# Attention, feed-forward and state-space block: weights in quarters, pinned statistics, an earlier decay rate, feed-forward tiles dealt out anew

## The chip, the cores and the metric

The kernel runs on one core of a Trainium2 chip. The metric is the device time of one execution in microseconds. The engines are TensorE (PE in the profile; PEld is its weight load), VectorE (DVE), ScalarE (ACT), GpSimd (POOL) and SyncE (SP), which issues every load and store of this kernel.

## The reference

Three residual branches are chained on x (4 x 256 x 512, so 1024 rows or eight tiles of 128), each behind a layer norm, and the feed-forward is used twice with the same weights:

```python
x = x + attention(_layernorm(x), w_attn, w_proj, adapter_wte, gating)
x = x + ffn(_layernorm(x), weight, bias, centroids, assignments)
x = x + mixer(_layernorm(x), in_proj_w, conv_w, conv_b, dt_bias, A_log, D, norm_w, out_w)
x = x + ffn(_layernorm(x), weight, bias, centroids, assignments)
```

The attention has 32 heads of 16 channels, rotary queries and keys, a causal softmax, and ten adapter keys with a softmax of their own, scaled by a gate. The feed-forward selects rows and columns by clusters:

```python
dots = softmax(x @ centroids.T / 0.1, axis=-1)      # 64 clusters
hits = dots > 0.01
query_sel = any(hits, axis=1)                       # rows
row_sel = any(hits, axis=0)[assignments]            # columns, over all 1024 rows
out = where(query_sel[:, None] & row_sel[None, :], x @ weight.T + bias, 0)
```

The mixer projects to a gate and to x (8192 channels each), to B and C (8 groups of 128) and to dt (128 heads), applies a causal convolution of four taps and silu, runs a state-space recurrence with the decay rates `A = -exp(A_log)`, gates, normalises in eight groups and projects back.

## The kernel before

Every large float32 product is made as three products of a high and a low part. `split` makes the parts: an ACT copy (line 104, "CAST" in the profile) gives the high part, and a subtraction (line 105) on DVE or POOL the low part. `mm3` issues the three matmuls (lines 112, 113 and 114) for each 128-row slice of the contraction. A normalised tile is made in three steps: `stats` (BN statistics and their aggregate on DVE), `root` (a square root on ACT, a reciprocal on DVE), then `scale` and `turn` (four transposes on PE, whose result is split into `axs`). ACT loads a function table whenever it passes from Sqrt to Exp or back; such loads are instructions of their own.

**Start.** SP loads x's tiles 0 and 1, the constants and the weights of q, k and v, each in two loads of 512 KB, then the rest of x, the gate, the adapter's rows `wte` and wproj. `weights` loads and splits one matrix, q and k with DVE's low parts, v with POOL's. Ten matmuls on a tile of ones run meanwhile (`warmed`). `rotated` makes the rotary embedding: three DVE products (lines 281, 284 and 285) and a POOL sum (line 287), then POOL stacks high and low parts (lines 305 and 306) and PE transposes them (trp). The statistics of tiles 2 to 7 and their common root stand next in the program.

**Attention's blocks.** A loop runs over i = 0 to 31, four batches of eight blocks of four heads. PE's order is written by hand (`tc.manual_schedule`), one block being: scores sc of block i, steps of the coroutines that are due, the weighted values py of block i-2, the transposes ptr of block i-1, the gathering of block i-3. Coroutines yield a kind ("long", "turn" or "values") and a due block, and `step(kind, i)` moves those that are due. The other engines' orders come from a list scheduler; `keep_in_program_order` holds an instruction behind the one before it in the program on its engine, `issue_after` holds what follows behind a given instruction of the same engine, and `high_priority` pulls an instruction forward. The exponentials of a block (line 461) are 16 ACT instructions.

**The first feed-forward** starts inside the loop. `Feed.tile` makes a tile's two halves pd (288 columns each; the first has the 64 cluster logits), takes the maximum (lines 206 and 207), the exponentials fe (209), the hit (212), the row's choice (213), the maximum into `hits` (214) and the new row (217 to 219). The dictionary `FEEDS` deals the tiles out: tiles 0 to 2 enter at blocks 28, 29 and 31. Tiles 3 to 5 follow the loop, and tiles 6 and 7, the `late` ones, the last output projections po. Then `select` counts the hits over the rows with a matmul (cnt), makes the mask (msk), and eight `take` copies (line 230) put the new rows into x.

**The mixer's start.** Weight blocks `win` are fetched ahead and split (w). The decay rates `a_s` are loaded, and ACT and DVE make -exp of them (lines 807 and 808). Takes, statistics and roots (mrs, line 140) alternate; ACT normalises (mxn, line 150) and PE transposes. Then come dt, its cumulative sums, and 64 blocks of projections pp, convolutions, state-space products and, group by group, output projections pog.

**The end.** The same `Feed` class, named g, runs on the tiles as their last pog products come in, then select, the takes and the stores of the output.

Of the kernel before, what the change touches and what calls it, by code (L numbers as in the profile page):

```python
# [9 lines left out]
F32 = mybir.dt.float32  # L10
F32R = mybir.dt.float32r
# [9 lines left out]
P = 128  # L21
# [56 lines left out]
def hybrid_kernel(  # L78
# [17 lines left out]
    nc.vector.memset(eps, EPS)  # L96
    ones = keep.tile([P, P], F32, name="ones")
# [74 lines left out]
    class Feed:  # L172
# [24 lines left out]
        def tile(self, t, xs, halves):  # L197

            p2 = self.p2
            pa, pb = halves  # L200
            for j, o in enumerate(halves):
                mm3(o, [[v[:, k, :] for v in xs] for k in range(KC)],
                    [[v[:, k, j, :] for v in self.w] for k in range(KC)])
            small = lambda n, w: p2.tile([P, w], F32, name=f"{self.name}{n}", tag=f"f{n}")
            nm = small("nm", 1)
            nc.vector.tensor_reduce(nm, pa[:, :NCL], AX.X, ALU.max, negate=True)
            nc.vector.tensor_scalar(nm, nm, 10.0, None, ALU.mult)
            e, se = small("e", NCL), small("se", 1)
            nc.scalar.activation(e, pa[:, :NCL], AF.Exp, bias=nm, scale=10.0, accum_out=se)
            nc.vector.reciprocal(se, se)  # L210
            hit, sel = small("hit", NCL), small("sel", 1)
            nc.vector.tensor_scalar(hit, e, se, 0.01, ALU.mult, ALU.is_gt)
            nc.vector.tensor_reduce(sel, hit, AX.X, ALU.max)
            nc.vector.tensor_tensor(self.hits, self.hits, hit, ALU.max)
            new = self.new[:, t, :]
            m = FH - NCL
            nc.vector.tensor_tensor(new[:, :m], pa[:, NCL:], self.bias[:, :m], ALU.add)
            nc.vector.tensor_tensor(new[:, m:], pb, self.bias[:, m:], ALU.add)
            nc.vector.scalar_tensor_tensor(new, new, sel, x[:, t, :], ALU.mult, ALU.add)

        def select(self, cnt, rows):

            nc.tensor.matmul(cnt, self.hits, ones, start=True, stop=True)
            csel = self.p2.tile([NCL, P], BF16, name=f"{self.name}c", tag="fc")
            nc.vector.tensor_scalar(csel, cnt, 0.5, None, ALU.is_gt)
            nc.tensor.matmul(rows, csel, self.onehot, start=True, stop=True)
            self.mask = rows.bitcast(U32)
# [5 lines left out]
    def attention(later):  # L233
        with ExitStack() as es:
# [19 lines left out]
            def weights(w, src, tag, engine, pool=p2):  # L254
                for k in range(0, KC, 2):
                    r = pool.tile([P, 2, C], F32, name="ar", tag=tag)
                    load(r, src[:, k : k + 2, :])
                    for j in range(2):
                        split([v[:, k + j, :] for v in w], r[:, j, :], engine)
# [316 lines left out]
            def finished(b, c, po):  # L576
# [7 lines left out]
                if b == B - 1 or c == 1:  # L584
                    feed.norm.root(t if b == B - 1 else t - 1, t + 1)

            def fed(f, t):
                yield "turn", None
                with tc.high_priority(offset=60):
                    xs = normed(f.norm, t)  # L590
                yield "long", None
                f.tile(t, xs, [ps.tile([P, FH], F32, name="pd", tag="m") for _ in range(2)])
# [3 lines left out]
            load(x[:, 1, :], xv[:, 1, :])  # L596
# [3 lines left out]
            warmed(ps.tile([P, C], F32, name="warm", tag="m"), [ones] * 10)  # L600
# [3 lines left out]
            )  # L604
            for t in range(2):
                norm.stats(t)
            norm.root(0, 2)
            weights(wq_s, wq, "pc0", nc.vector)
# [5 lines left out]
            load(wte_s, wte)  # L614
            nc.gpsimd.tensor_copy(identb, ident)
# [17 lines left out]
            FEEDS = {28: 0, 29: 1, 31: 2}  # L633
# [18 lines left out]
            for t in range(2, TT):  # L652
                norm.stats(t)
# [8 lines left out]
            with tc.manual_schedule(engines={nc.tensor.engine}):  # L662
                for i in range(n):
# [8 lines left out]
                    if i in FEEDS:  # L672
                        moved(fed(feed, FEEDS[i]), i - 1)
                    if i == 3:
# [66 lines left out]
                late = {}  # L741
                for c, po in enumerate(pos):
                    t = 2 * b + c
                    finished(b, c, po)
                    late[t] = p2.tile([P, C], F32, name="axn", tag="t1")
                    feed.norm.scale(t, late[t])
                step("long", n + 3)
                for t, xn in late.items():
                    tr = ps.tile([P, KC, P], F32, name="tr", tag="m")
                    xs = [p2.tile([P, KC, P], F32R, name=f"axs{j}", tag=f"axs{j}") for j in range(2)]  # L750
                    feed.norm.turn(xn, tr, xs)
                    feed.tile(t, xs, [ps_s.tile([P, FH], F32, name="pd", tag="sc") for _ in range(2)])
# [4 lines left out]
    def mixer(feed, later):  # L757
        with ExitStack() as es, ExitStack() as inner:
# [8 lines left out]
            nc.gpsimd.memset(w0.tile([P, 8], F32, name="fill0"), 0.0)  # L767
# [37 lines left out]
            a_s = w1.tile([P, 1], F32, name="a_s")  # L805
            load(a_s, alog)
            nc.scalar.activation(a_s, a_s, AF.Exp)
            nc.vector.tensor_scalar(a_s, a_s, -1.0, None, ALU.mult)
# [7 lines left out]
            nc.gpsimd.memset(w1.tile([P, 32], F32, name="fill1"), 0.0)  # L816
# [488 lines left out]
```

## Time and profile before

| | us |
|---|---|
| median of 3 runs | 1895.22 |
| lowest and highest | 1891.03, 1895.73 |
| the profiled execution | 1896.1 |
| its span, first to last instruction | 1894.3 |
| PE busy | 1816.5 (96%) |
| DVE busy | 1465.8 (77%) |
| ACT busy | 1367.5 (72%) |
| POOL busy | 389.9 (21%) |

The times are device times of whole executions. The profile shows one of them, which took 1896.1; its span is 1.8 us shorter than its time. The page has the busy time of each engine, the span in forty slices with the clock that TensorE was granted, the chain of work that ended last, and groups of instructions. In the timeline, a row is start, length, engine, line, operation, output<-inputs, shapes and count; the bracket is the engine's idle time before it and what ended it. A window's row gives the busy time of every engine in a stretch and its granted clock, 1.00 being full speed.

### The profile page before, as it was taken

The page shows a single profiled execution, that of the slowest core. Times are in us where ns is not written, and L with a number is a line of the kernel's source. Part 1 is how long each engine was busy: PE and PEld are TensorE (multiplying, and loading weights), DVE is VectorE, ACT ScalarE, POOL GpSimd, SP SyncE. Part 2 cuts the span into 40 slices and gives each one's busy share as a digit, 9 for nine tenths or more (in the row PEclk, how much of TensorE's full clock was granted, in tenths as well). Part 3 has the DMA queues.
Part 4 walks back from the last instruction along what each step waited for, and adds up shares of the span by engine and source line. Part 5 has one row for each costly group of instructions (what it writes and reads, how often), then busy time and mean ns, then how long its engine had stood idle before and what let it go on. Part 6 is the DMA issues. An engine that isn't in the chain of part 4 may idle for free.

```text
span 1894.3 us, 29853 instructions
## 1 busy us (share of the span) xinstructions
PE 1816.5 (96%) x10690; PEld 1453.2 (77%) x10690; DVE 1465.8 (77%) x2319; ACT 1367.5 (72%) x2808; POOL 389.9 (21%) x380
## 2 busy tenths in 40 slices
PE   7999988799999999999999999999999999999997
PEld 6777767676777877877788778777787888787786
DVE  5566666688998778777877787778878877877777
ACT  4666675468998768777877787778777876786753
POOL 5432230011311212211112111211221221122100
PEclk8999999999999999999999999999999999999999
DMA  4000000125555454544544454545454545455341
GB/s 135 8 1 1 22 15 1 32 70 180 168 183 189 148 160 148 171 152 156 174 150 147 144 187 146 172 145 167 151 167 145 160 152 168 146 162 164 112 124 49
DMA packets 151908, 240.34 MB, mean 127 GB/s; under 512 B 12368, under 2 KB 77520, under 8 KB 151760
## 3 DMA queue, kind: packets, MB, share of 16 engines
q1 hardware_dynamic: 151760, 238.44, 39.4%
q8 instruction: 84, 1.38, 0.3%
q14 instruction: 64, 0.52, 0.1%
HBM read 202.75 MB, written 35.65 MB: 126 GB/s over the span
## 4 chain that ended last, share of the span: by engine, by line
PE 76%; ACT 8%; DVE 8%; DMA 3%; issue 3%; POOL 1%; SPq 0%; DVEq 0%; ACTq 0%; POOLq 0%
PE pp L112 12%; PE pp L113 11%; PE pp L114 11%; PE pyy L1021 8%; PE pog L112 6%; PE pog L114 6%; PE pog L113 6%; PE trx L1006 3%; ACT e L461 2%; DMA wor<-in_wout_dram 2%; DVE acc L947 1%; PE ptr L477 1%; PE pq L112 1%; PE pq L113 1%; PE pq L114 1%
## 5 line engine op out<-in xcount | busy, mean ns | idle before, releaser
L112 PE MATMUL pp<-mx,w 128*128 128x512 f32 (+1 forms) x1160 | 465.2, 401 | 8.1 <-DVE acc L947 7.6
L114 PE MATMUL pp<-mx,w 128*128 128x512 f32 (+1 forms) x1160 | 453.8, 391 | 0.0
L113 PE MATMUL pp<-mx,w 128*128 128x512 f32 (+1 forms) x1160 | 453.6, 391 | 0.0
L947 DVE SCALAR_TENSOR_TENSOR acc<-pp,cw_s,acc 128x1012 f32<-128x1012 f32 (+2 forms) x240 | 304.9, 1270 | 22.8 <-ACT acc L940 22.2
L995 DVE TENSOR_TENSOR em<-em,gm 128x1536 f32<-128x1536 f32 x128 | 227.9, 1780 | 94.4 <-ACT em L989 86.0
L112 PEld LDWEIGHTS pp<-mx,w 128*128 128x128 f32 x1160 | 218.3, 188 | 65.6 <-issue 10.4
L114 PEld LDWEIGHTS pp<-mx,w 128*128 128x128 f32 x1160 | 218.3, 188 | 45.4 <-issue 0.4
L1044 POOL TENSOR_TENSOR sq<-sq,acc 128x1024 f32<-128x1024 f32 x55 | 132.7, 2412 | 581.0 <-ACT acc L1043 581.0
L983 POOL TENSOR_SCALAR_AFFINE_SELECT r<-r 128x512 f32<-128x512 f32 x128 | 141.5, 1106 | 532.1 <-DMA r<-cumd 452.2
L113 PEld LDWEIGHTS pp<-mx,w 128*128 128x128 f32 x1160 | 218.5, 188 | 40.8 <-issue 0.7
L104 ACT CAST w<-wr 128x512 fp32r<-128x512 f32 x144 | 88.4, 615 | 186.9 <-PE pp L113 148.1
L112 PE MATMUL pog<-wo,gh 128*128 128x512 f32 x512 | 204.5, 399 | 0.0
L988 ACT ACTIVATE em<-r,col_t 128x128 f32<-128x128 f32 x512 | 165.0, 391 | 48.9 <-PE pyy L1021 46.8
L114 PE MATMUL pog<-wo,gh 128*128 128x512 f32 x512 | 200.2, 391 | 0.0
L113 PE MATMUL pog<-wo,gh 128*128 128x512 f32 x512 | 199.9, 390 | 0.0
L1021 PE MATMUL pyy<-em,xd 128*64 128x256 f32 (+1 forms) x2048 | 189.1, 329 | 3.2 <-DVE em L995 3.2
L1021 PEld LDWEIGHTS pyy<-em,xd 128*64 128x64 f32 x2048 | 134.0, 137 | 64.6 <-issue 21.4
L991 ACT ACTIVATE em<-r,col_t 128x128 f32<-128x128 f32 x512 | 166.5, 388 | 0.0
L979 DVE TENSOR_SCALAR em<-r,col_t 128x128 f32<-128x128 f32 x512 | 137.1, 327 | 12.6 <-PE pyy L1021 10.1
L1007 DVE TENSOR_TENSOR xd<-trx,dt_t 128x512 f32<-128x512 f32 x128 | 86.2, 682 | 54.4 <-PE trx L1006 54.2
L105 DVE TENSOR_TENSOR w<-wr,w 128x512 fp32r<-128x512 f32 x139 | 99.0, 713 | 34.3 <-ACT w L104 34.3
L461 ACT ACTIVATE e<-sc,nmx 128x256 f32<-128x256 f32 (+1 forms) x256 | 104.2, 442 | 20.8 <-DVE nmx L455 20.7
(287 smaller groups left out, 3193.0 us busy)
## 6 DMA issues: line engine op xcount, KB each, us to landing
wr<-in_win_dram SPq DMA_DIRECT2D x287, 256.0 KB, 2.8
r<-cumd SPq DMA_DIRECT2D x128, 512.0 KB, 4.1
spill<-gb SPq DMA_DIRECT2D x63, 512.0 KB, 2.8
gr<-spill SPq DMA_DIRECT2D x120, 256.0 KB, 3.5
wor<-in_wout_dram SPq DMA_DIRECT2D x64, 256.0 KB, 3.3
out_dram<-x SPq DMA_DIRECT2D x8, 256.0 KB, 2.3
x<-in_x_dram SPq DMA_DIRECT2D x1, 1536.0 KB, 10.9
gr<-spill SPq DMA_DIRECT2D x8, 192.0 KB, 2.8
```

The lines of the kernel that those rows point to most:

```text
L112: nc.tensor.matmul(o, lh, rh, start=(first and k == 0), stop=False)
L113: nc.tensor.matmul(o, lh, rl, start=False, stop=False)
L114: nc.tensor.matmul(o, ll, rh, start=False, stop=(last and k == n - 1))
L461: nc.scalar.activation(es_[c][:, 2 * j + pr, :], sc[:, j, :], AF.Exp, bias=nm[:, j : j + 1], accum_out=rs[:, c, h : h + 1],)
L947: nc.vector.scalar_tensor_tensor(av[:, :, d:], pv[:, :, : L - d], cw_s[:, ch, tap : tap + 1], av[:, :, d:], ALU.mult, ALU.add,)
L979: nc.vector.tensor_scalar(e[:, b, 2, :], rv[:, b, 1, :], col_t[:, h, b, 1:2], 0.0, ALU.subtract, ALU.min,)
L983: nc.gpsimd.affine_select(rv[:, :, 0, :], rv[:, :, 0, :], pattern=[[0, B], [1, P]], compare_op=ALU.is_ge, fill=-1e30, base=0, channel_mult ...
L988: nc.scalar.activation(e[:, b, 1, :], rv[:, b, 1, :], AF.Exp, bias=col_t[:, h, b, 2:3])
L991: nc.scalar.activation(e[:, b, 0, :], rv[:, b, 0, :], AF.Exp, bias=col_t[:, h, b, 0:1])
L995: nc.vector.tensor_tensor(e, e, gm, ALU.mult)
L1021: nc.tensor.matmul(py[d, b, k * P :], xd[:, 2 * b + k, d], es2[hh][:, b, 2 * k : 2 if k == 0 else 3, :].rearrange("p s i -> p (s i)"), sta ...
L1044: (nc.gpsimd if n < NB - 1 else nc.vector).tensor_tensor(sq, sq, x2, ALU.add)
```

## The change

The weights of q, k and v are loaded in quarters of 256 KB, q's ahead of x's tile 1. Sixteen warming matmuls stand for ten. Tiles 0 and 1 have a root each. The statistics of tiles 2 to 7 are held behind what precedes them on DVE, the rotary products. The decay rates are loaded with the first weights and made in block 2 (the negation on POOL). Feed tiles 0 to 2 enter with their products at blocks 30, 31 and 32, without priority. `Feed.tile` is cut in two, `products` and `chosen`. Of tiles 6 and 7 both roots come ahead of tile 5's exponentials, and tile 7's transposes lie between the halves of tile 6. The last tile's hit is no longer merged into `hits`; a second matmul adds it to the count. The small fillers keep their sum of 40 columns.

```diff
@@ class Feed
         def tile(self, t, xs, halves):
+            for j in range(2):
+                self.products(xs, j, halves[j])
+            self.chosen(t, halves)
+
+        def products(self, xs, j, o):
+            mm3(o, [[v[:, k, :] for v in xs] for k in range(KC)],
+                [[v[:, k, j, :] for v in self.w] for k in range(KC)])
+
+        def chosen(self, t, halves):
             p2 = self.p2
             pa, pb = halves
-            for j, o in enumerate(halves):
-                mm3(o, [[v[:, k, :] for v in xs] for k in range(KC)],
-                    [[v[:, k, j, :] for v in self.w] for k in range(KC)])
...
             nc.vector.tensor_scalar(hit, e, se, 0.01, ALU.mult, ALU.is_gt)
+            if t < TT - 1:
+                nc.vector.tensor_tensor(self.hits, self.hits, hit, ALU.max)
+            else:
+                self.last = hit
             nc.vector.tensor_reduce(sel, hit, AX.X, ALU.max)
-            nc.vector.tensor_tensor(self.hits, self.hits, hit, ALU.max)
...
-            nc.tensor.matmul(cnt, self.hits, ones, start=True, stop=True)
+            nc.tensor.matmul(cnt, self.hits, ones, start=True, stop=False)
+            nc.tensor.matmul(cnt, self.last, ones, start=False, stop=True)
@@ attention: weights
                     r = pool.tile([P, 2, C], F32, name="ar", tag=tag)
-                    load(r, src[:, k : k + 2, :])
+                    if pool is p1:
+                        load(r, src[:, k : k + 2, :])
                     for j in range(2):
+                        if pool is not p1:
+                            load(r[:, j, :], src[:, k + j, :])
                         split([v[:, k + j, :] for v in w], r[:, j, :], engine)
@@ attention: finished, fed
                 if b == B - 1 or c == 1:
-                    feed.norm.root(t if b == B - 1 else t - 1, t + 1)
+                    return feed.norm.root(t if b == B - 1 else t - 1, t + 1)
...
                 yield "turn", None
-                with tc.high_priority(offset=60):
-                    xs = normed(f.norm, t)
-                yield "long", None
+                xs = normed(f.norm, t)
+                yield "long", max(0, B * 8 + t - 2)
@@ attention: the start
             load(x[:, 0, :], xv[:, 0, :])
-            load(x[:, 1, :], xv[:, 1, :])
...
-            warmed(ps.tile([P, C], F32, name="warm", tag="m"), [ones] * 10)
+            warmed(ps.tile([P, C], F32, name="warm", tag="m"), [ones] * 16)
...
+            weights(wq_s, wq, "pc0", nc.vector)
+            load(x[:, 1, :], xv[:, 1, :])
             for t in range(2):
                 norm.stats(t)
-            norm.root(0, 2)
-            weights(wq_s, wq, "pc0", nc.vector)
+                norm.root(t, t + 1)
...
             load(wte_s, wte)
+            load(a_s, alog)
...
-            FEEDS = {28: 0, 29: 1, 31: 2}
+            FEEDS = {28: 0, 29: 1, 30: 2}
...
             for t in range(2, TT):
-                norm.stats(t)
+                norm.stats(t, tc.keep_in_program_order)
...
+                    if i == 2:
+                        nc.scalar.activation(a_s, a_s, AF.Exp)
+                        nc.gpsimd.tensor_scalar(a_s, a_s, -1.0, None, ALU.mult)
@@ attention: after the loop
-                late = {}
+                xns, xss = {}, {}
                 for c, po in enumerate(pos):
                     t = 2 * b + c
-                    finished(b, c, po)
-                    late[t] = p2.tile([P, C], F32, name="axn", tag="t1")
-                    feed.norm.scale(t, late[t])
-                step("long", n + 3)
-                for t, xn in late.items():
+                    rooted = finished(b, c, po)
+                    xns[t] = p2.tile([P, C], F32, name="axn", tag="t1")
+                    feed.norm.scale(t, xns[t])
+
+                def turned_late(t):
                     tr = ps.tile([P, KC, P], F32, name="tr", tag="m")
-                    xs = [p2.tile([P, KC, P], F32R, name=f"axs{j}", tag=f"axs{j}") for j in range(2)]
-                    feed.norm.turn(xn, tr, xs)
-                    feed.tile(t, xs, [ps_s.tile([P, FH], F32, name="pd", tag="sc") for _ in range(2)])
+                    xss[t] = [p2.tile([P, KC, P], F32R, name=f"axs{j}", tag=f"axs{j}") for j in range(2)]
+                    feed.norm.turn(xns[t], tr, xss[t])
+
+                with tc.issue_after(rooted):
+                    step("long", n + 3)
+                turned_late(TT - 2)
+                halves = {t: [ps_s.tile([P, FH], F32, name="pd", tag="sc") for _ in range(2)] for t in xns}
+                feed.products(xss[TT - 2], 0, halves[TT - 2][0])
+                turned_late(TT - 1)
+                feed.products(xss[TT - 2], 1, halves[TT - 2][1])
+                feed.chosen(TT - 2, halves[TT - 2])
+                feed.tile(TT - 1, xss[TT - 1], halves[TT - 1])
@@ mixer
-            a_s = w1.tile([P, 1], F32, name="a_s")
-            load(a_s, alog)
-            nc.scalar.activation(a_s, a_s, AF.Exp)
-            nc.vector.tensor_scalar(a_s, a_s, -1.0, None, ALU.mult)
```

More of the change, by code (lines that the diff above doesn't have):

```diff
@@ L96, in hybrid_kernel @@
     nc.vector.memset(eps, EPS)
+    a_s = keep.tile([P, 1], F32, name="a_s")
     ones = keep.tile([P, P], F32, name="ones")
@@ L766, in mixer @@
             rg_s = [w0.tile([P, TT], F32, name=f"rg{i}") for i in range(2)]
-            nc.gpsimd.memset(w0.tile([P, 8], F32, name="fill0"), 0.0)
             po_ = pool("mo", 2, **freed)
@@ L815, in mixer @@
             load(nw_s, nw)
-            nc.gpsimd.memset(w1.tile([P, 32], F32, name="fill1"), 0.0)
+            nc.gpsimd.memset(w1.tile([P, 40], F32, name="fill1"), 0.0)
             dh = w1.tile([P, NB], F32, name="dh")
```

## The prediction

> **What bounds the kernel now.** I read the summary first, then the forty slices with the granted TensorE clock, then the chain that ended last, and then, stage by stage, the windows table and the timeline of the few microseconds around each moved instruction.
>
> ```profile
> span 1894.3 us, 29853 instructions
> ...
> PE   7999988799999999999999999999999999999997
> ...
> PEclk8999999999999999999999999999999999999999
> ...
> PE 76%; ACT 8%; DVE 8%; DMA 3%; issue 3%; POOL 1%; SPq 0%; DVEq 0%; ACTq 0%; POOLq 0%
> ```
>
> TensorE (PE) is the bound. It is below 90% in the first slice, in slices 6 to 8 (about 237 to 379 us: attention's last blocks, the feed-forward, the mixer's start) and in the last. Over three quarters of the chain is PE, and from 400 to 1800 us it never starves (last row below). The change leaves the mixer's 64 blocks nearly alone: three neighbouring pairs swap order there. So it can win only in five places: start, blocks 28 to 32, end of attention, start of the mixer, last feed-forward. In four of them PE idles now and then runs on a halved clock (columns: window, length, busy time of PE, PEld, DVE, ACT, POOL with counts, granted clock, DMA share, GB/s):
>
> ```profile
> 316.60:320.00 3.40, 1.33 (x9) 0.62 (x6) 3.40 (x8) 3.40 (x18) 0.00 (x0) 1.00 0.00 0
> 320.10:326.80 6.70, 5.73 (x23) 5.51 (x24) 2.30 (x10) 1.32 (x4) 1.40 (x3) 0.50 0.00 0
> 358.00:364.60 6.60, 5.17 (x25) 4.94 (x26) 2.25 (x6) 2.68 (x6) 0.00 (x0) 0.74 0.01 2
> 374.70:388.30 13.60, 10.09 (x37) 7.83 (x37) 8.76 (x25) 8.83 (x14) 3.05 (x4) 0.50 0.21 58
> 400.00:1000.00 600.00, 589.41 (x3225) 469.32 (x3224) 506.20 (x686) 480.82 (x864) 126.74 (x84) 1.00 0.50 161
> ```
>
> PE was busy for 1.33 of 3.40 us, and the clock was 0.50 in the next two windows, where a 128x288 product takes 0.24 us a step instead of 0.13.
>
> **Part by part.**
>
> *Start (quarters, pinned statistics, decay rates): -2 us, between -3.5 and +1.* Now q's four ACT casts (615 ns each) follow two 512 KB loads, and the first q product starts at 11.43 behind ACT's axs. With quarters only one cast follows the last landing: axs comes near 10.2. The third wk product now stands early in PE's order, so about 0.5 to 1 us of this is kept. The wv loads go out at about 10.7 instead of 11.81, and POOL's wv halves end near 20.8 instead of 22.43. From there POOL's rotary sums are the chain:
>
> ```profile
> 29.93 1.27 POOL L287 TENSOR_TENSOR r<-t,t 128x512 f32<-128x512 f32 x1 [0.72 <-DVE t L285]
> ```
>
> The fourth sum waited 0.72 us for DVE, where three BN statistics (0.66 us each) had slipped in ahead of it; pinned, all six come behind it. The sum should start near 27.5. What is added in front of ACT's first exponentials (38.49 now): an Exp table load plus a_s, then two wp casts (1.2 us), then a Sqrt table load (1.28). ACT idled 2.50 us in that place, waiting for a transpose, and the root cannot run before the sixth statistic (near 32) anyway, so I cost them at nothing; without that cover they cost 1.2 + 1.28 = 2.5. One added wait deserves a name: those two casts wait for the load of wproj, which SP issues once DVE has made wt's low half (31.84 to 32.55 now, issue at 32.57, 3.6 us to landing). Behind them on ACT stand the root, the last key casts and all exponentials. In the new order wt's low half runs ahead of the fourth rotary product, near 25, so wproj lands near 29.5, before the casts' turn. Six more issues on SP cost 0.43 us each, beside transfers in flight; a_log's issue goes ahead of wproj's, beside that wait. POOL's negation of a_s (128x1) is put at 0.2 us ahead of the fourth sum, by DVE's 0.15 for the same operation now.
>
> A rule speaks against the quarters: the Trainium skill (DMA: Bandwidth & Descriptors, Bandwidth) says to batch transfers to 1 MiB or more, giving 32% efficiency at 64 KB and 78% at 1 MB. Put 256 KB midway at 55% of its 425 GB/s and 512 KB at 66% (my estimates from that page): 3 MiB then take 13.5 instead of 11.2 us, 2.3 lost, and the start is worth nothing. In the trace, queued transfers overlap: a 2 KB packet takes 84 ns, a 4 KB one 159, so two halves cost 5.7% more, about 0.4 us over 3 MB. I go by the packets; the rule sets the upper end.
>
> *Blocks 29 to 32 (feed tiles 0 to 2 at blocks 30, 31, 32): -3.5, between -6 and +1.*
>
> ```profile
> 321.07 0.61 PE L112 MATMUL pd<-fw,axs 128*128 128x288 f32 x1 [2.21 <-ACT axs L104]
> ...
> 355.22 1.28 ACT L209 ACT_TABLE_LOAD   x1 [3.41 <-DVE fnm L207]
> ...
> 359.05 0.40 PE L112 MATMUL pd<-fw,axs 128*128 128x288 f32 x1 [2.83 <-ACT axs L104]
> ...
> 371.21 0.40 PE L223 MATMUL cnt<-ones,fh 128*64 128x128 f32 x2 [1.47 <-DVE fh L214]
> ```
>
> Tile 0's 24 products (297.5 to 300.7) leave block 29, and block 30's exponentials come about 2.3 us earlier (306.90 to 304.6); block 31's come 3.0 earlier (316.74 to 313.8). Tile 1's 3.2 us of products now lie in block 31, where PE is busy 1.33 of 3.40. Tile 2's products then start near 319: with a full clock they end 4.8 us earlier than today's 327.2, on a cold one 2. Between them I take 3.5. The other table loads stay under DVE's maxima. Beyond that, pd holds two of the three "m" buffers until DVE reads them; ptr and try stand behind it, hence the bad end.
>
> *End of attention (roots of tiles 6 and 7 together, tile 7's transposes inside tile 6's products, last hit apart): -4.2, between -5.5 and -1.5.* On ACT now: Exp table, fe of tile 5 (356.52), Sqrt table (356.94 to 358.22), root 7, then axs of tile 6 at 358.43, for which PE waited 2.83 us since the transposes at 355.62. With both roots first, axs of tile 6 comes one table load earlier, 357.4 (-1.0). Later the Exp table load (362.43) and fe 6 stood before tile 7's axs (365.20), which now follows its transposes, put between the halves of tile 6; that and a PE gap short enough to keep the clock (1.5 us were lost at 0.24 a step) make pd7 end at 365.6 instead of 369.7. The maximum into hits (1.11 us, in line ahead of cnt) leaves the chain, for one extra accumulating matmul (0.2 us): about -0.5 more, less if the clock stays halved. Take of tile 0: 372.5 to about 368.
>
> *Start of the mixer (decay rates gone): -2.5, between -3.5 and -1.*
>
> ```profile
> 374.52 1.28 ACT L807 ACT_TABLE_LOAD   x1
> ...
> 377.06 1.28 ACT L140 ACT_TABLE_LOAD   x1
> ...
> 379.41 1.97 PE L163 MATMUL tr<-con,mxn 128*128 128x128 f32 x8 [2.50 <-ACT mxn L150]
> ```
>
> Between tile 0's root (374.21) and tile 1's (378.36) ACT does: Exp table 1.28, a_s 0.20, two w casts 1.12, Sqrt table 1.28. Without the first, second and fourth 2.76 us go, and tile 0's normalisation moves ahead of one cast. Late next: the cast of w's second half and DVE's takes, 0.7 us each; hence 2.5.
>
> For these four table loads the Trainium skill (ScalarE: Activation LUTs, What ACT_TABLE_LOAD costs) names 1283 ns and another 1380 for a drain, 2.66 in all. By that the four are worth 10.6 us. The trace shows 1.28 and the next ACTIVATE within 0.02 us (378.34 to 378.36), so I count 5.1, within the two parts above; the page would make the sum 5.5 us better.
>
> *Last feed-forward: +0.3, between -0.7 and +2.5.* The scheduler, fed the new pieces, puts tile 6's transposes behind 23 of tile 5's 24 products (now behind three) and both roots ahead of fe 5. ACT: roots, Exp table (1875.24 to 1876.52), fe 5, and only then gxs of 6 and 7, near 1876.95 and 1877.55. PE has nothing between 1876.85 and 1877.5 and little until DVE's low half near 1878.2: 48 products end some 0.6 later. The last hit saves a reduction and a maximum (0.21 each) ahead of cnt, less one matmul. The extra Sqrt/Exp pair earlier lies under PE's pog products, which have no gap there; uncovered it is 2.6, the upper end.
>
> *Sum.* -2 - 3.5 - 4.2 - 2.5 + 0.3 = -11.9. Five stages do not all land, and I hold back 0.7 for the moved clock windows. The profiled run took 1896.1 (span 1894.3 and 1.8 around it): 1896.1 - 11.2 = 1884.9. It stands 0.9 above the median of the runs, so the median comes to 1884.0, 0.6% less.
>
> **Rivals.** *Half of it is taken back (chance 0.13).* The halved clock comes in stretches of 3.41 us or multiples (320.05 to 326.88, 374.67 to 388.32). If moving the gaps only moves those stretches, block 32 gains 1, the end of attention 2, the mixer 1.5, and the start nothing (wproj's landing or wk's quarters): -4.5, so 1890.7. For: the four places are each next to a gap. Against: three of the gaps shrink by more than a table load.
>
> *The clock of the attention blocks (0.05, slower).* From 45 to 293 us PE pauses in every block, yet only four of some 73 such windows are halved (50.4, 105.0, 258.6, 275.7). Starting 2 us earlier shifts every block against that grid. A halved window costs at most 1.7 us. If ten more are halved the loss is 17, and with the rest of the change -11 + 17 = +6: 1901. It decides from about seven more, which just cancel the gain. For: the three runs, 4.7 us apart. Against: a shift finds as many good phases as bad.
>
> *It does not do what it says (0.01).* The compiled order of each engine does show the quarters, the roots and the vanished mixer tables; what is left is a stage where another wait ends last: no change, 1895.
>
> **How the numbers follow.** About 0.3% (5.7 us) is what a measurement here can tell from no change, so faster means under 1889.5. The likeliest case, 0.81, gives 1884, from 1876 (all five near their good ends, -18 or so) to 1890. The first rival adds 0.12 to no change and a little to faster, the second gives the slower 0.05. Faster 0.82, same 0.13, slower 0.05. Range 1876.5 to 1891.5: it takes in the first rival's middle and leaves out the second and the extremes.
>
> **What would show it.** First exponentials near 36.5; block 31's near 312 with the start's gain; no ACT table load between fe of tile 5 and axs of tile 6; first mixer product 7.7 us behind the first take, instead of 9.5; gxs of tile 6 after fe 5 at the end, with 0.5 to 1.5 us of PE idle. Wrong: ACT idle before the wp casts on wproj; clock 0.50 in more windows before 290; a PE row before pd of tile 2 still waiting for axs over 2 us.

## The result and the profile after

The changed kernel takes 1882.56 us (median of 4 runs, 1881.00 to 1883.73); the kernel before takes 1894.89 beside it (1891.03 to 1895.73). The ratio is 0.9938 with a 95% interval of 0.9921 to 0.9956: 12 us or 0.6% faster. The forecast was 1884.0. On another occasion (experiment 9) the ratio was 0.9938 again, 0.9920 to 0.9956. The two profiled executions, 1896.1 and 1881.0, are 15 us apart, so this one pair of profiles overstates the gain by about 3 us. Part of that lies where nothing was changed to gain time: the stretch from the first 128x512 mixer product to the last mixer block takes 2.2 us less after (1394.65 against 1396.81), and over the fourteen profiles of this case it takes anything from 1394.2 to 1398.9.

The lines of the page after that answer to those shown of before:

```profile
span 1879.2 us, 29896 instructions
...
PE   7999988899999999999999999999999999999997
...
PEclk9999999899999999999999999999999999999999
...
PE 79%; DVE 9%; ACT 7%; issue 2%; DMA 2%; POOL 1%; SPq 0%; DVEq 0%; ACTq 0%; POOLq 0%
```

Where it went is best read from a few events found in both traces (us from the start of the span):

| event | before | after | shift |
|---|---|---|---|
| first exponentials, block 0 | 38.49 | 35.52 | -3.0 |
| exponentials of block 3 | 66.45 | 66.22 | -0.2 |
| exponentials of block 29 | 295.45 | 294.52 | -0.9 |
| exponentials of block 30 | 306.90 | 303.56 | -3.3 |
| exponentials of block 31 | 316.74 | 312.67 | -4.1 |
| first product of feed tile 5 | 352.44 | 346.65 | -5.8 |
| first take | 372.52 | 361.58 | -10.9 |
| first mixer product | 382.06 | 369.63 | -12.4 |
| first 128x512 mixer product | 401.75 | 388.98 | -12.8 |
| last mixer block (POOL's square) | 1798.56 | 1783.63 | -14.9 |
| last mask | 1885.29 | 1869.96 | -15.3 |

The three gaps in front of PE, in the timeline after:

```profile
317.57 0.40 PE L113 MATMUL pd<-fw,axs 128*128 128x288 f32 x1
```

```profile
349.83 1.28 ACT L216 ACT_TABLE_LOAD   x1
351.13 0.31 ACT L216 ACTIVATE fe<-pd,fnm 128x64 f32<-128x64 f32 x1
...
352.06 0.41 PE L113 MATMUL pd<-fw,axs 128*128 128x288 f32 x1 [1.62 <-ACT axs L105]
```

```profile
367.84 0.48 PE L164 MATMUL tr<-con,mxn 128*128 128x128 f32 x1 [1.44 <-ACT mxn L151]
```

Tile 2's products no longer wait (2.21 us before). Tile 6's wait 1.62 instead of 2.83, with one table load ahead of axs instead of two. The mixer's second group of transposes waits 1.44 for ACT, where the first waited 2.50. The windows of the same stages (length, busy time of PE, PEld, DVE, ACT and POOL with counts, granted clock, DMA share, GB/s):

```profile
316.00:320.00 4.00, 3.10 (x24) 3.07 (x25) 3.63 (x14) 0.77 (x4) 0.46 (x1) 1.00 0.00 0
320.00:327.00 7.00, 5.62 (x52) 4.22 (x50) 6.13 (x16) 2.57 (x6) 0.90 (x2) 1.00 0.09 25
350.75:354.16 3.41, 1.87 (x12) 1.63 (x13) 2.63 (x8) 1.24 (x4) 0.00 (x0) 1.00 0.00 0
354.16:357.58 3.42, 3.42 (x26) 3.22 (x26) 2.50 (x10) 0.88 (x3) 0.00 (x0) 1.00 0.00 0
361.00:364.40 3.40, 1.84 (x4) 0.60 (x4) 3.30 (x8) 1.14 (x4) 0.35 (x2) 1.00 0.38 99
364.40:367.85 3.45, 2.01 (x7) 0.85 (x5) 2.62 (x6) 2.55 (x5) 2.87 (x4) 0.50 0.25 76
367.85:371.30 3.45, 2.67 (x9) 1.97 (x10) 3.45 (x10) 0.88 (x2) 0.00 (x0) 0.50 0.24 81
```

Block 31 now fills PE for 3.10 of 4.00 us, and the clock stays at 1.00 to 327, where it was 0.50 from 320 to 327. The fourth row is tile 6's and 7's products at full clock. Of these stages only the mixer's start still runs at 0.50, from 364.4 on.

### The profile page after: what moved, and what is told of

Same layout as the page of the kernel before. It is cut to its first block, busy times and chain, and to the rows that moved or that the text cites. A ratio compares the mean times of both kernels' runs of the same rounds, so it can differ in the third digit from the quotient of the medians.

```text
span 1879.2 us, 29896 instructions
## 1 busy us (share of the span) xinstructions
PE 1812.6 (96%) x10706; PEld 1450.4 (77%) x10706; DVE 1464.7 (78%) x2317; ACT 1367.7 (73%) x2809; POOL 397.0 (21%) x380
## 4 chain that ended last, share of the span: by engine, by line
PE 79%; DVE 9%; ACT 7%; issue 2%; DMA 2%; POOL 1%; SPq 0%; DVEq 0%; ACTq 0%; POOLq 0%
PE pp L113 12%; PE pp L114 12%; PE pp L115 12%; PE pyy L1043 9%; PE pog L113 6%; PE pog L115 6%; PE pog L114 6%; PE trx L1028 3%; ACT e L475 2%; DVE acc L969 2%; PE ptr L491 1%; DMA wor<-in_wout_dram 1%; PE pq L113 1%; PE pq L114 1%; PE pq L115 1%
## 5 line engine op out<-in xcount | busy, mean ns | idle before, releaser
L113 PEld LDWEIGHTS pp<-mx,w 128*128 128x128 f32 x1160 | 218.4, 188 | 65.7 <-issue 10.2
L1005 POOL TENSOR_SCALAR_AFFINE_SELECT r<-r 128x512 f32<-128x512 f32 x128 | 148.6, 1161 | 521.9 <-DMA r<-cumd 394.8
L1029 DVE TENSOR_TENSOR xd<-trx,dt_t 128x512 f32<-128x512 f32 x128 | 86.3, 684 | 54.1 <-PE trx L1028 53.9
```

What stands on the lines that cost most here:

```text
L113: nc.tensor.matmul(o, lh, rh, start=(first and k == 0), stop=False)
L1005: nc.gpsimd.affine_select(rv[:, :, 0, :], rv[:, :, 0, :], pattern=[[0, B], [1, P]], compare_op=ALU.is_ge, fill=-1e30, base=0, channel_mult ...
```

## The experiments

The kernels differ from the kernel before or from the changed kernel in the lines shown. Ratios are to the kernel before, measured beside them. The working theory when they were made: each stage pays by itself, and what the start wins is lost again by block 3 to the halved clock.

**1. The start alone.** The kernel before with the start's edits, without the decay rates (q's loads also go ahead of x's tile 1, as in the change):

```diff
-                    load(r, src[:, k : k + 2, :])
                     for j in range(2):
+                            load(r[:, j, :], src[:, k + j, :])
...
-            warmed(ps.tile([P, C], F32, name="warm", tag="m"), [ones] * 10)
+            warmed(ps.tile([P, C], F32, name="warm", tag="m"), [ones] * 16)
...
-            norm.root(0, 2)
+                norm.root(t, t + 1)
...
-                norm.stats(t)
+                norm.stats(t, tc.keep_in_program_order)
```

> The kernel before with the start alone changed: quarters, load order, a root per tile, sixteen warming products, pinned statistics; no early decay rates. Theory: the start gains about 3 us at block 0's first exponentials (38.5 to about 35.5) and loses nearly all of it by block 3's (66.5 to 66.0 or later), because the gap in block 1 to 2 falls whole into one clock window and two windows are then halved (46.98 to 53.8) instead of one; total 0 to -1 us. Rival: the gain travels to the end, total -2 to -3 us, as the prediction counted it.

Measured: 1891.74, ratio 0.9991 (0.9984 to 0.9998), so -1.7 us. First exponentials at 35.97, block 3's at 67.44. The interval, -3.0 to -0.4, takes in the prediction's -2 and the theory's -1 as well.

**2. The decay rates alone.**

```diff
+            load(a_s, alog)
...
+                    if i == 2:
+                        nc.scalar.activation(a_s, a_s, AF.Exp)
+                        nc.gpsimd.tensor_scalar(a_s, a_s, -1.0, None, ALU.mult)
...
-            load(a_s, alog)
-            nc.scalar.activation(a_s, a_s, AF.Exp)
-            nc.vector.tensor_scalar(a_s, a_s, -1.0, None, ALU.mult)
```

> The kernel before with the decay rates alone moved from the mixer's start to the attention. Theory: -1.5 to -2.5 us between the first take and the steady blocks, nothing at the start as long as ACT has idle time there; total about -2. Rival: the two table loads added at the start delay the first exponentials by 1.3 to 2.6 us and give it back; total 0.

Measured: 1892.04, ratio 0.9996 (0.9988 to 1.0005), so -0.8 and not to be told from nothing. First exponentials at 35.98, at the early end of the 35.68 to 38.49 that the old start shows without the edit: no sign of the rival's delay, though a spread of 2.8 us could hide one. From the first take to the first mixer product it takes 7.32 us instead of 9.54.

**3. Feed tiles alone.**

```diff
-            FEEDS = {28: 0, 29: 1, 31: 2}
+            FEEDS = {28: 0, 29: 1, 30: 2}
...
-                with tc.high_priority(offset=60):
-                    xs = normed(f.norm, t)
-                yield "long", None
+                xs = normed(f.norm, t)
+                yield "long", max(0, B * 8 + t - 2)
```

> The kernel before with feed tiles 0 to 2 dealt to blocks 30, 31 and 32, without priority. Theory: -2.4 us by block 30's exponentials, -3 by block 31's, and another 2 from tile 2's products on a full clock, so that py after them comes 5 to 6 us earlier; total -5. Rival: the clock in block 32 depends on the phase that the start gave in the full change, tile 2's products stay on the halved clock here, total -3.

Measured: 1888.21, ratio 0.9974 (0.9962 to 0.9985), so -4.9. From block 29's exponentials to tile 5's first product it takes 52.15 us, in the changed kernel 52.13, before 56.99. Tile 2's products run at full clock although the start is as before, so the rival falls.

**4. The late tiles alone**: both roots first, tile 7 turned inside tile 6, the hit still merged.

```diff
+                with tc.issue_after(rooted):
+                    step("long", n + 3)
+                turned_late(TT - 2)
...
+                feed.products(xss[TT - 2], 0, halves[TT - 2][0])
+                turned_late(TT - 1)
+                feed.products(xss[TT - 2], 1, halves[TT - 2][1])
```

> The kernel before with only tiles 6 and 7 re-dealt: both roots ahead of tile 5's exponentials, tile 7's transposes inside tile 6's products; the last hit is still merged. Theory: tile 6's products start 1.2 us earlier and tile 7's run on a full clock right behind, the count comes about 4 us earlier (371.2 to about 367); total -4. Rival: without the saved 1.1 us of the merged hit and with the window's phase of before the clock stays halved through tile 6 and 7, total -2.

Measured: 1890.14, ratio 0.9983 (0.9975 to 0.9991), so -3.2. From tile 5's first product to the first take: 17.32 us instead of 20.08. The clock was halved behind tile 6's wait, as the rival had it, and the stage gave -2.8.

**5. The last hit alone.**

```diff
+            if t < TT - 1:
+                nc.vector.tensor_tensor(self.hits, self.hits, hit, ALU.max)
+            else:
+                self.last = hit
...
+            nc.tensor.matmul(cnt, self.last, ones, start=False, stop=True)
```

> The kernel before with the last tile's hit kept apart and added by a second count matmul, and products and chosen as two functions; nothing else. Theory: about 1 us earlier at the first count, and about 0.4 us less from the last group's sums to the last mask, since the late gxs of tile 6 costs less than the reduction and the maximum that go; total -1.2. Rival (the prediction): the late gxs of tile 6 costs 0.5 us or more in the last feed-forward, total -0.5 or nothing.

Measured: 1891.84, ratio 0.9997 (0.9989 to 1.0006). The stage to the first take shrinks by 1.0 us (19.09 against 20.08). From the last mixer block to the last mask it takes 86.88, before 86.73. The time cannot tell -0.6 from nothing, and the 0.4 that the theory expected at the end did not come. This edit alone brings the new order of the last feed-forward.

**6. Everything but the start**, the edits of experiment 1 taken out of the changed kernel:

```diff
-            warmed(ps.tile([P, C], F32, name="warm", tag="m"), [ones] * 16)
+            warmed(ps.tile([P, C], F32, name="warm", tag="m"), [ones] * 10)
...
-                norm.stats(t, tc.keep_in_program_order)
+                norm.stats(t)
```

> The changed kernel with the start as before (weights in halves, ten warming products, one root for both tiles, statistics not pinned); early decay rates, feed tiles, late tiles and last hit as changed. Theory: block 3's exponentials come at the same time as in the changed kernel within 1 us, and the total is within 1 us or so of the changed kernel (1882 to 1884 if that is 1882.5). Rival: the start's -2 of the prediction stays, total 2 to 3 us longer than the changed kernel.

Measured: 1883.69, ratio 0.9957 (0.9945 to 0.9969). The changed kernel's 0.9938 was measured at other times, so the start's share here, 0.0019 or 3.6 us, is uncertain by about 4; experiment 7, measured beside it, took 1.8 less. First exponentials at 37.07, block 3's at 67.45.

**7. A filler in block 1.**

```diff
+                py = ps_y.tile([P, L], F32, name="warm", tag="py")
                 for q in range(4):
+                    warmed(py, [ones] * 2)
```

> The changed kernel with two extra 128x128 products on the tile of ones ahead of each of the four groups of adapter key transposes in block 1, into the values' PSUM buffer that is free there: about 1.5 us more of PE work in a stretch where PE idles for over 2 of 3.4 us. Their results are used by nothing. Theory: the clock window from 43.6 to 47.0 counts as busy, the halved stretch from 47.0 goes or is cut to one window, and block 3's exponentials come 1 to 2 us earlier than in the changed kernel; total -1 to -2. Rival: block 2 is bound by the chain of POOL stacks, ACT key copies and transposes, and block 3 comes at the same time or 0.3 later.

Measured: 1881.86, ratio 0.9945 (0.9932 to 0.9958), the changed kernel's time. The changed kernel's clock was halved at 46.96, behind a window in which PE was busy for 1.18 of 3.42. Here the windows lie 1.4 us later:

```profile
44.91:48.32 3.41, 2.32 (x21) 1.95 (x19) 1.06 (x3) 3.26 (x17) 3.12 (x8) 1.00 0.01 2
48.32:51.73 3.41, 3.41 (x18) 2.64 (x17) 0.00 (x0) 0.45 (x2) 2.06 (x6) 0.50 0.02 5
```

The filler brought PE to 2.32 us, and the clock was halved all the same, for two windows as before. Block 3's exponentials came at 68.38, 30.9 us behind the first, where the changed kernel took 30.7. The theory falls, and since the clock was not kept, the run does not settle what binds block 2.

**8. A filler at the mixer's start.**

```diff
+            warmed(ps.tile([P, C], F32, name="warm", tag="m"), [ones] * 4)
...
-                        warmed(ps.tile([P, C], F32, name="warm", tag="m"), [x[:, t, :]])
+                        warmed(ps.tile([P, C], F32, name="warm", tag="m"), [x[:, t, :]] + [ones] * (4 * t))
```

> The changed kernel with eight more 128x128 products on the tile of ones at the mixer's start, four beside the mask's matmul and four behind the warming product of tile 1, whose results are used by nothing. Theory: the window in which PE now is busy for about half stays above the point at which the clock is halved, the three halved windows after the first takes (364.4 to 374.7 in the changed kernel) shrink to at most one, and the steady blocks start 2 to 3 us earlier; total -2. Rival: DVE's takes and statistics and ACT's normalisation set this stretch, PE gets its clock back and waits instead, total 0.

Measured: 1885.48, ratio 0.9967 (0.9954 to 0.9980), no gain and perhaps a loss. Its windows:

```profile
361.00:364.40 3.40, 3.00 (x16) 1.84 (x15) 3.27 (x8) 1.28 (x1) 1.26 (x1) 1.00 0.22 66
364.40:367.85 3.45, 2.84 (x15) 1.74 (x14) 2.58 (x8) 2.32 (x5) 2.27 (x2) 1.00 0.13 37
367.85:371.30 3.45, 1.19 (x6) 0.71 (x6) 3.45 (x8) 1.88 (x3) 0.85 (x3) 0.94 0.56 150
371.30:374.70 3.40, 2.83 (x13) 2.83 (x14) 3.33 (x10) 1.73 (x3) 0.00 (x0) 0.50 0.31 77
```

The clock is full to 371, as the theory wanted. But DVE is busy for 3.27, 2.58, 3.45 and 3.33 us of each window, PE then idles for two thirds of the third one, and the halved stretch comes two windows later. There it lies on PE's products: behind the first mixer product the clock is halved for 6.8 us, where it was 5.0 in the changed kernel. Experiments 7, 10, 11 and 12 show the same late stretch without this filler, so it may be no more than where the windows fell. From the first take to the first 128x512 product it takes 28.20 us (27.40 after). No gain, as the rival had it; what the products would be worth at full clock, the run does not show.

**9. The changed kernel again**, with no edit, beside experiments 10 to 12.

> The changed kernel itself, beside the next three on one chip, and as a second profile of it. If the 1.3 us that tile 7's products took less in the first profile than in the three other kernels with the same order was the phase of the clock windows, this profile may show either; its first exponentials lie anywhere in 35 to 37.5, and block 3's within 1 us of 66.2 whatever they are. Total 0.9935 to 0.995 of the kernel before.

Measured: 1880.53, ratio 0.9938 (0.9920 to 0.9956). First exponentials at 35.58, block 3's at 66.36, 14.94 us from tile 5's first product to the first take: the first profile again, to within 0.15 us.

**10. A filler in front of tile 6.**

```diff
+                warmed(ps_y.tile([P, L], F32, name="warm", tag="py"), [ones] * 6)
                 feed.products(xss[TT - 2], 0, halves[TT - 2][0])
```

> The changed kernel with six 128x128 products on the tile of ones put on PE between tile 6's transposes and its products, into the values' PSUM buffer, free by then; nothing uses them. They fall in the 1.6 us in which PE waits for axs of tile 6. Theory: with that gap filled the clock is not halved behind it, tile 6's first products to the count take 7.8 us in every run, where three kernels took 9.1; total 0 to -1 against the changed kernel, by as often as it was halved. Rival: the window after it is halved all the same, or PE is late for tile 6 by the filler; total 0 to +1.

Measured: 1882.59, ratio 0.9947 (0.9932 to 0.9963): the same as experiment 9 within the intervals. The window that holds the wait, now with the filler in it, is busy for 2.91 us, and the next keeps its clock:

```profile
348.93:352.35 3.42, 2.91 (x21) 2.48 (x21) 2.34 (x9) 0.88 (x3) 0.00 (x0) 1.00 0.00 0
352.35:355.76 3.41, 3.41 (x26) 3.20 (x25) 2.79 (x10) 0.88 (x3) 0.00 (x0) 1.00 0.00 0
```

PE is not late by the filler (14.93 us to the first take). That the filler kept the clock is not shown: this window began 4.5 us behind tile 5's first product, and in the two profiles of the changed kernel, where it began 4.1 behind, the clock was kept without one. The halved cases began 3.1 to 3.9 behind. Its worth cannot be more than the 1.3 us that a halved window costs, in those runs in which it falls, and the times do not show it.

**11. Statistics not pinned.**

```diff
-                norm.stats(t, tc.keep_in_program_order)
+                norm.stats(t)
```

> The changed kernel with the statistics of tiles 2 to 7 free to go ahead of the fourth rotary product, as before; wt's low half, wproj's load and the first two wp casts go back behind the first exponentials with them. Theory: POOL's fourth rotary sum starts 0.7 us later behind the third, first exponentials within 1 us of the changed kernel's, and block 3 at the same time; total 0 to +0.5. Rival (the prediction): the pin is a part of a 2 us gain at the start that travels; total +1.

Measured: 1881.57, ratio 0.9943 (0.9927 to 0.9958). First exponentials at 35.10, block 3's at 63.06, 3.3 earlier than in experiment 9, with one halved window between them instead of two. In the time, the pin gives nothing that can be measured.

**12. Weights in halves.**

```diff
-                            load(r[:, j, :], src[:, k + j, :])
+                    load(r, src[:, k : k + 2, :])
```

> The changed kernel with the weights of q, k and v in 512 KB halves again; everything else of the start as changed. Theory: the last q cast and with it axs of tile 0 come about 1 us later, the first exponentials too, and block 3 comes within 0.5 us of the changed kernel; total 0 to +0.5. Rival (the prediction): wv's earlier issue and split carry 1.2 to 1.6 us to the end; total +1 to +1.5. Rival by the page on DMA: halves are faster than quarters, total -1 or less.

Measured: 1886.45, ratio 0.9967 (0.9954 to 0.9980), 5.9 us more than experiment 9's median, with intervals that touch, and more than any of the expectations. Experiment 8 has the same ratio with the changed start, so not all of it need be the start's. In the profile the start travels: first exponentials 2.3 us later than in experiment 9 (37.88), block 3's 1.8 later (68.11), block 29's 2.5 later (297.19). Another 1.3 comes from a halved window at tile 7:

```profile
352.44:355.85 3.41, 1.56 (x11) 1.08 (x10) 2.62 (x10) 2.25 (x5) 0.00 (x0) 1.00 0.00 0
355.85:359.27 3.42, 3.42 (x17) 3.40 (x16) 1.26 (x5) 0.64 (x3) 0.00 (x0) 0.50 0.00 0
```

The kernel with halves is not faster, so the rival falls. But this run does not compare the loads alone. ACT's order changed with them: both casts of wv's first half now stand behind axs of tile 1,

```profile
15.72 0.59 ACT L105 CAST axs<-tr 128x512 fp32r<-128x512 f32 x1 [2.66 <-PE tr L164]
16.20 2.18 ACT L105 CAST wv<-ar 128x512 fp32r<-128x512 f32 x4
```

although that half had landed at 13.17. In the changed kernel two of wv's casts go first:

```profile
13.61 1.29 ACT L105 CAST wv<-ar 128x512 fp32r<-128x512 f32 x2
15.18 0.58 ACT L105 CAST axs<-tr 128x512 fp32r<-128x512 f32 x1 [0.27 <-PE tr L164]
```

POOL's low halves of wv end at 22.03, in the changed kernel at 19.82, and POOL's rotary sums follow them.

The stages side by side, from one profile of each kernel (us):

| kernel | first exponentials | block 3 | block 29 to tile 5 | tile 5 to first take | take to first mixer product | take to first 128x512 product | last block to last mask |
|---|---|---|---|---|---|---|---|
| before | 38.49 | 66.45 | 56.99 | 20.08 | 9.54 | 29.23 | 86.73 |
| after | 35.52 | 66.22 | 52.13 | 14.93 | 8.05 | 27.40 | 86.33 |
| 1 start | 35.97 | 67.44 | 56.13 | 20.05 | 9.14 | 28.71 | 86.73 |
| 2 rates | 35.98 | 66.24 | 57.18 | 20.07 | 7.32 | 26.93 | 86.71 |
| 3 feeds | 37.16 | 66.61 | 52.15 | 19.75 | 9.39 | 28.48 | 86.78 |
| 4 late | 35.68 | 65.65 | 55.80 | 17.32 | 9.54 | 28.19 | 86.78 |
| 5 hit | 36.28 | 67.06 | 56.67 | 19.09 | 9.54 | 28.10 | 86.88 |
| 6 no start | 37.07 | 67.45 | 52.08 | 16.26 | 7.79 | 28.26 | 86.66 |
| 7 filler, block 1 | 37.45 | 68.38 | 52.07 | 14.93 | 7.45 | 27.72 | 87.16 |
| 8 filler, mixer | 35.25 | 65.91 | 52.17 | 16.35 | 7.63 | 28.20 | 86.31 |
| 9 changed again | 35.58 | 66.36 | 52.17 | 14.94 | 8.01 | 27.44 | 86.26 |
| 10 filler, tile 6 | 35.74 | 65.31 | 52.18 | 14.93 | 7.52 | 27.57 | 86.26 |
| 11 unpinned | 35.10 | 63.06 | 52.11 | 16.26 | 7.46 | 27.96 | 87.04 |
| 12 halves | 37.88 | 68.11 | 52.17 | 16.27 | 7.45 | 27.90 | 86.83 |

## Why the prediction was right

The sum was -11.2 and the medians gave -12.3. By time alone, the five parts give -1.7, -0.8, -4.9, -3.2 and -0.6, together -11.2, so the parts add up to the whole (-11.7 by its ratio) within the intervals. That the sum came this close is in part luck, since two terms missed in opposite directions. Step by step:

*Start, forecast -2: the events came, what they are worth is not settled.* They came as worked out or earlier: axs of tile 0 at 8.69 (10.2 forecast), the fourth rotary sum at 26.96 (27.5), SP's issue of wproj at 24.69 and no wait of the wp casts for it, POOL's negation 0.22 us, first exponentials at 35.52 (36.5). The decay rates, put into the program at block 2, in fact run before block 0 (Exp at 21.85, negation at 26.78). Their two table loads and the wp casts, costed at nothing, found just enough cover: ACT runs without a pause from 29.86 to 35.52, and its last casts, at 33.14, begin while their transposes (32.23 to 33.55) still run. But one step has the wrong cause: with halves again (experiment 12) axs of tile 0 came at 8.86, so it is not the quarters that bring it forward. What is left is q's place ahead of x's tile 1 and the root of its own, which were not tried apart, nor were the sixteen warming products.

The kernel before also has a start that varies, 35.68 to 38.49 us to the first exponentials with weights in halves and the old order (the kernel before and experiments 2 to 6), and the forecast was worked out from the latest of these. Most of the -3.0 in the table of events is that one late start. Six profiles of the old start and six of the new (after, experiments 1 and 7 to 10) have means of 36.78 and 35.92 at the first exponentials, 66.58 and 66.60 at block 3, 294.76 and 294.26 at block 29. So on the means 0.9 is won at block 0, nothing is left at block 3 and 0.5 at block 29, each uncertain by about 1. How long blocks 0 to 3 take goes with the clock: 27.96 us in the two profiles with one halved window there (before, experiment 11), 29.5 to 30.9 in the eleven with two, 31.5 in the one with three (experiment 1). By time the start is worth 1.7 alone (0.4 to 3.0), 3.6 by leaving it out (uncertain by 4) and 5.9 by the halves, which include more than the start. It is likely a gain; -2 is neither confirmed nor excluded.

*The rule on transfer size.* The Trainium skill's advice of 1 MiB transfers (DMA: Bandwidth & Descriptors, Bandwidth) made the start worth nothing, by my estimate of 20% more per byte for quarters; the packet times made it -2. The landings are with the packets: wk's quarters landed at 10.95, 11.58, 12.27 and 12.94 in the changed kernel, 0.66 us apart, its halves at 10.61 and 11.90 in experiment 12, 1.29 apart, so a quarter costs 3% more per byte. The page's figures are for loads issued from GpSimd; these are issued by SP. Still, wk's last quarter landed 1.0 later than its last half: the quarters did not win by landing sooner.

*Blocks 29 to 32, forecast -3.5: too small by about 1.* Block 30's and 31's exponentials moved as forecast (-2.4 and -3.1 against block 29's; -2.3 and -3.0 forecast). The step that was mis-sized is tile 2's products on a clock taken halfway between full (4.8 us earlier) and halved (2): they ran at full clock in the changed kernel and in experiment 3, without the other edits. The stage takes 52.1 to 52.2 us in all nine profiles with the edit, and 55.8 to 57.2 in the five without: -4.4 on the means, -4.9 by time.

*End of attention, forecast -4.2: right, between two cases.* From tile 5's first product to the first take it is -3.8 when the window behind tile 6's wait is halved (16.3 us) and -5.1 when it is not (14.9). Late tiles alone gave -2.8 and the hit -1.0 in this stage, with the clock halved; by time the two gave -3.2 and -0.6.

*Start of the mixer, forecast -2.5: too large.* The first mixer product came 8.05 us behind the first take (7.7 forecast), and table loads cost 1.28 us with nothing behind them, so the extra drain that the Trainium skill names (ScalarE: Activation LUTs, What ACT_TABLE_LOAD costs) does not show here either. No load is saved in all, the two profiles have 195 each: the loads moved to where ACT had time. The means over the kernels without and with the edit are 9.43 and 7.63 at the first product, -1.8, just what the forecast's own sign of 9.5 to 7.7 says; the 2.5 in the sum was 0.7 more than that, and named DVE's takes as late next without giving them room. Then more is lost. At the first 128x512 product the means are 28.54 and 27.71: only -0.8 is left, outside the range of -3.5 to -1, and the edit alone gave -0.8 by time. What failed is that PE's first product carries the rest along. Between the two, PE issues the same 120 matmuls and is busy for 17.9 and 18.0 us on the means, but it idles for 1.23 without and 2.06 with the edit. The next normalisations wait for DVE as before (the first line is before, the second after):

```profile
383.76 1.52 ACT L150 ACTIVATE mxn<-x,mmv,mrs 128x512 f32<-128x512 f32 x2 [1.01 <-DVE mmv L145]
```

```profile
371.94 1.52 ACT L151 ACTIVATE mxn<-x,mmv,mrs 128x512 f32<-128x512 f32 x2 [1.04 <-DVE mmv L146]
```

They start 11.2 and 10.4 us behind the first take, so 0.9 of the gain is left there. From the first take to 373.5 DVE is busy for 10.9 of 11.9 us.

*Last feed-forward, forecast +0.3: nothing.* The order is as forecast, but the wait is not:

```profile
1859.84 1.28 ACT L216 ACT_TABLE_LOAD   x1
...
1861.43 1.06 ACT L105 CAST gxs<-tr 128x512 fp32r<-128x512 f32 x2
...
1862.06 0.40 PE L113 MATMUL pd<-gw,gxs 128*128 128x288 f32 x1 [0.39 <-DVE gx L227]
```

PE pauses 0.39 us, for a buffer that DVE reads late, and not the 0.5 to 1.5 us for gxs. The stage takes 86.3 to 87.2 us with the new order and 86.7 to 86.8 with the old.

The rivals: the halved clock did take something back, 1.3 us in some runs at tile 7; attention's other blocks did not slow down. So the blocks' term, 0.9 to 1.4 us too small, and the mixer's, 1.7 too large, nearly cancel, beside a start whose worth is uncertain by about as much.

## What to carry to other kernels

A table load or a wait that goes is worth what the engine at the end of the stage can use: the same 2.76 us of ACT bought 1.8 at the next product and 0.8 twenty microseconds on, because the matmul engine then waited 0.8 longer for a chain that begins on a nearly full DVE. One profile shows the order of events well and their distances to within a microsecond or two; where an edit is to be worth 2 us, the same stage in several kernels that share its code tells more than one pair of traces. An edit that makes a scheduler deal anew is not a test of one thing: the halves of experiment 12 also moved two casts on ACT. And work dealt into a stretch in which the matmul engine idled paid twice here, by the work and by the clock behind it (experiment 3).

## What was not expected of the hardware

Where the clock windows lie decides whether a wait costs a halved window. The stretch of 3.41 us that holds tile 6's wait has the same instructions in the changed kernel and in experiments 6, 8, 11 and 12, and differs by where the windows lie. With PE busy for 1.87 and 1.91 us in it (the changed kernel, twice) the next window kept its clock. With 1.56 to 1.60 (the four experiments) the next was halved.

It looks like an edge near half of a window, but PE's busy time in the profile does not give one. In the changed kernel itself a window with 2.00 us was followed by a halved one:

```profile
272.24:275.65 3.41, 2.00 (x14) 1.21 (x14) 2.11 (x6) 3.35 (x17) 0.00 (x0) 1.00 0.00 0
275.65:279.06 3.41, 3.41 (x28) 2.65 (x30) 2.81 (x7) 1.49 (x5) 1.03 (x3) 0.50 0.02 5
```

So was the one from 361.0 to 364.4, with 1.84. Counted over the windows at full clock from 40 to 400 us in the fourteen profiles, 1327 of them, all that were busy for less than 1.81 us were followed by a halved one and none above 2.37; between the two, both happen (1.81 kept its clock in experiment 10, and 2.37 lost it in experiment 7). So in these traces a filler could only be relied on above about 2.4 of 3.41 us.
